# Turning gathered expert rows by DMA transposes of 16-bit halves in a four-layer attention and mixture-of-experts kernel

## The chip, the cores and the metric

The kernel runs on one core of one Trainium2 chip. The metric is the device time of one execution in microseconds (us), taken as the median of three runs. The profile is one further execution, recorded by the hardware profiler.

## The reference

Four layers act on x (8 batches of 256 tokens of width 256), each as x = x + layer(layernorm(x)). The first two are a correlation attention and a feed-forward layer with assigned experts, the third is a cross attention. The change lies wholly in the fourth, a mixture of 8 experts of inner width 1024 with the two best experts per token and a shared expert beside them:

```python
probs = jax.nn.softmax(logits, axis=-1)
top_v, top_i = jax.lax.top_k(probs, K)          # K = 2 of 8 experts
gates = jnp.zeros((T, e)).at[jnp.arange(T)[:, None], top_i].set(top_v)
g = jax.nn.silu(jnp.einsum('td,edf->etf', flat, w1_e))
u = jnp.einsum('td,edf->etf', flat, w3_e)
out_e = jnp.einsum('etf,efd->etd', g * u, w2_e)
routed = jnp.einsum('te,etd->td', gates, out_e).reshape(b, s, d)
return 0.5 * shared + 0.5 * routed
```

Everything is 32-bit float.

## The kernel before

**The mixture's stages.** While the third layer runs, each token's normalised row, its 8 gates and its own number (a row of `ROW` = 265 words) are sent by indirect DMA into the table `Td` in DRAM, sorted by expert. The mixture then works through `NBLK` = 11 blocks in one loop (L3796). Blocks 0 and 1 are the shared expert on two groups of 512 tokens, blocks 2 to 9 are the experts 0 to 7 with up to 512 rows each, and block 10 is the shared expert on the last group. Rows of an expert beyond 512 are worked on by the generator `slots` (L3598), one step of which is put between two units, from (2,1) on until it is done.

**Units.** A block is four up units, called (b,0) to (b,3) below, and one down unit. The order is (b,0), the down unit of block b-1, (b,1), (b,2), (b,3), then (b+1,0). Each unit is a product of 2 by 2 blocks in seven multiplications instead of eight, in three accumulators in PSUM: `a`, `e` (two buffers each) and `B` (two). `run_unit` (L3407) writes out the order by hand. TensorE's seven steps are A11 into a, S1 into e, then the *last* step of the unit before it (A22 into that unit's a, in `end_open`, L3399), S2 into a, A12 into B, S4 into e, S3 into a. Between them stand the reads: ScalarE's copies `seed` (L3221), `read_p5` and `read_u2`; VectorE's sums `read_c12` and `read_c22` (L3255) into the tile `cc`; and, after the A22 step, VectorE's `mult_2` (L3271), `read_last` (L3276) and `act_sums` (L3173) on the unit before. The lists `early`, `amid`, `late` and `after` are further steps that `run_unit` places after the A22 step, after A12, after S4 and after S3.

**Order of the engines.** The whole part stands under a manual schedule (L1256): every engine, SP's DMA queue included, runs its instructions in the order of the program. Waits are put in by the framework: an instruction that rewrites a buffer waits for all that still read it, and a DMA counts as reading until it has completed.

**Rows of an expert.** `load_rows` (L3489) loads the 512 rows of an expert into `R` (one buffer, 128 partitions by 4 rows by 265 words) through SP. `Turned` (L3497) turns them round, so that the width lies on the partitions: `half(kc)` does four TensorE transposes of 128x128 into PSUM (L3509) and one ScalarE copy to the tile `RT` (L3512). After the first half VectorE copies the token numbers into `ids` (L3514) and the gates into `gts` (L3515), both with three buffers. `Rows.steps` (L3146) then makes four sums of blocks of `RT` on VectorE. All of this lies in the down unit of block b-1, for the block n = b+1, and for expert 0 in unit (1,3).

**Result of an expert.** The down unit of an expert, `RoutedDown` (L3347), scales its four groups of 128 rows by the gates into `Y` and adds each to the output in DRAM, `Od`, by an accumulating indirect DMA that GpSimd issues (`add_rows`, L3517), with a column of `ids` as row numbers. The adds of groups 0 and 1 are issued in `read_c12` of the down unit, those of groups 2 and 3 in `read_last`, which comes in unit (b,1). As all write `Od`, each waits for the one before it to complete.

**Weights.** `load_up` (L2903) and `load_down` (L2921) load an expert's weights through SP, into tiles with two buffers each; `load_slots` (L3582) loads quarters of the weights for `slots`. The sums of the weights lie in parts of two older tiles: `SW` in the front of `HP` (L3758) and `TW` in the first six rows of `X` (L3761). The rows `lrows` of `X` (the last group of tokens) have been stored to `Od` before the loop (L3711) and are read back in block 10 (L3847).

Of the kernel before, what the change touches and what calls it, by code (L numbers as in the profile page):

```python
# [9 lines left out]
F32 = mybir.dt.float32  # L10
BF16 = mybir.dt.bfloat16
U32 = mybir.dt.uint32
I32 = mybir.dt.int32
AF = mybir.ActivationFunctionType
ALU = mybir.AluOpType
# [4 lines left out]
P = 128  # L20
LN_EPS = 1e-5
CAP1 = 576
FIRST = 512
# [1063 lines left out]
def fast_path(  # L1087
# [33 lines left out]
    nc = tc.nc  # L1121
    B, S, D = x.shape
    T = B * S
    NT = T // P
    KC = D // P
    TPB = S // P
    E = L0_ffn_w1.shape[0]
# [22 lines left out]
    X = res.tile([P, NT, D], F32, name="X")  # L1150
# [3 lines left out]
    ROW = D + E + 1  # L1154
# [13 lines left out]
    ident = const.tile([P, P], F32, name="ident")  # L1168
# [93 lines left out]
    pm = l0.enter_context(tc.tile_pool(name="pm", bufs=2))  # L1262
# [34 lines left out]
    for dst, src, i in (  # L1297
# [12 lines left out]
        out=bqd.rearrange("o (b c) -> (o b) c", b=B),  # L1310
        in_=L0_xattn_bq.partition_broadcast(B),
    )
    nc.scalar.dma_start(
        out=WZ[:, :, DH : 2 * DH],
        in_=L0_xattn_Wq.rearrange("(kc p) c -> p kc c", p=P),
# [267 lines left out]
    for h in range(TPB):  # L1583
# [36 lines left out]
        out=tri,  # L1620
        in_=tri,
# [26 lines left out]
    for sign, base in ((1, 1), (-1, 16)):  # L1648
        nc.gpsimd.affine_select(
            out=rows_f,  # L1650
            in_=rows_f,
# [33 lines left out]
    for r in range(2):  # L1685
        (nc.sync if r == 0 else nc.scalar).dma_start(
            out=Gd[0, 0 : S * W2].rearrange(
                "(tt p r w) -> p tt r w", p=P, r=2, w=S
            )[:, :, r, :],
            in_=G,  # L1690
# [4 lines left out]
        out=DG,  # L1695
        in_=Gd[0, :].rearrange("(tt p w) -> p tt w", p=P, w=W2 + 1)[:, :, 1 : S + 1],
# [53 lines left out]
    for tt in range(2):  # L1750
# [3 lines left out]
    rest = pa.tile([P, S], F32, name="rest")  # L1754
# [4 lines left out]
        out=rest, in_to_replace=top[:, 0, :], in_values=pcorr, imm_value=-3.0e38  # L1759
# [16 lines left out]
        out=Wd[:, 0:W2].rearrange("o (r s) -> o r s", r=2),  # L1776
        in_=wrow.unsqueeze(1).to_broadcast([P, 2, S]),
# [4 lines left out]
        out=CW,  # L1782
        in_=bass.AP(wd.tensor, wd.offset + P - 1, [[WD - 1, P], [P, 2], [1, S]]),
# [186 lines left out]
    sums = pa.tile([P, NT, 2], F32, name="sums")  # L1970
# [50 lines left out]
    halves = [slice(m * S, (m + 1) * S) for m in range(2)]  # L2021
# [7 lines left out]
    b = order_b  # L2029
# [101 lines left out]
    def load_row(e):  # L2131
# [14 lines left out]
        out=Yd.rearrange("(c p) d -> p c d", p=P),  # L2146
        in_=blank[:, 0:D].unsqueeze(1).to_broadcast([P, NT, D]),
# [300 lines left out]
    for e in range(E - 1):  # L2448
        if e == 5:

            wpv = L1_xattn_Wp.rearrange("(c g m d) n -> m g d c n", c=NB, g=4, m=2)
            for m in range(2):
                for g in range(4):
# [3 lines left out]
                        out=bvc[r0 : r0 + DH, :],  # L2457
                        in_=bkv[:, 1, :].rearrange("(c g m) d -> m g d c", c=NB, g=4)[m, g],
# [70 lines left out]
    ps_m = banks.enter_context(tc.tile_pool(name="ps_m", bufs=3, space=PSUM))  # L2529
# [436 lines left out]
    for b in range(B):  # L2966
        for c in range(NB):
# [55 lines left out]
            if prev is None:  # L3023
# [12 lines left out]
                HP = pg1.tile([P, NT, ROW], F32, name="HP")  # L3036
# [20 lines left out]
    FULL = FIRST // P  # L3057
# [7 lines left out]
    lrows = slice(LAST * (TB // P), NT)  # L3065
    HT2 = TB // 2
    HF = F // 2
# [17 lines left out]
    class UpWeights:  # L3085


        def __init__(self, wab, sums, s1=None):
            self.sums = sums
            self.raw = {  # L3090
                (h, kc): wab[:, :, kc, h * HF : (h + 1) * HF]
                for h in range(2)
                for kc in range(KC)
            }
            self.part = {
                A11: self.raw[0, 0],
                A12: self.raw[0, 1],
                A22: self.raw[1, 1],
                S1: self.raw[1, 0] if s1 is None else s1,
                S3: sums[:, :, 0],  # L3100
                S2: sums[:, :, 1],
                S4: sums[:, :, 2],
            }
# [120 lines left out]
    class Up(Unit):  # L3224
        n = TB
# [56 lines left out]
    class Down(Unit):  # L3282
        n = HT2
# [123 lines left out]
    def run_unit(u, early=(), amid=(), late=(), after=()):  # L3407

        before = open_unit[0]
        u.mm(u.a, A11, "b11", True)  # L3410
        u.seed()
        if before is not None:
            before.silu_2()
        u.mm(u.e, S1, "t1", True)
        u.read_p5()
        end_open()
        for do in early:
            do()
        u.mm(u.a, S2, "t2")
        u.read_u2()  # L3420
        u.mm(u.b, A12, "b21")
        for do in amid:
            do()
        u.mm(u.e, S4, "b22")
        u.read_c12()
        for do in late:
            do()
        u.mm(u.a, S3, "t3")
        u.read_c22()
        for do in after:  # L3430
            do()
        open_unit[0] = u
# [56 lines left out]
    def load_rows(e):  # L3489
        R = pe2.tile([P, FULL, ROW], F32, tag="R", name="R", bufs=1)  # L3490
        nc.sync.dma_start(
            out=R,
            in_=Td[e * CAP1 : e * CAP1 + FIRST, :].rearrange("(r p) w -> p r w", p=P),
        )
        return R

    class Turned:  # L3497


        def __init__(self, e, R):  # L3500
            self.e, self.R = e, R
            self.RT = pe2.tile([P, KC, FIRST], F32, tag="RT", name="RT")
            self.ids = pe2.tile([P, FULL], U32, tag="ids", name="ids", bufs=3)
            self.gates = pe2.tile([P, FULL], F32, tag="gts", name="gts", bufs=3)

        def half(self, kc):
            pt = ps_m.tile([P, FULL, P], F32, tag="pm", name="pt")
            for r in range(FULL):
                nc.tensor.transpose(  # L3509
                    pt[:, r, :], self.R[:, r, kc * P : (kc + 1) * P], ident  # L3510
                )
            nc.scalar.copy(self.RT[:, kc, :], pt.rearrange("p r q -> p (r q)"))  # L3512
            if kc == 0:
                nc.vector.tensor_copy(self.ids, self.R[:, :, ROW - 1])  # L3514
                nc.vector.tensor_copy(self.gates, self.R[:, :, D + self.e])  # L3515

    def add_rows(Y, ids):  # L3517
        nc.gpsimd.indirect_dma_start(  # L3518
# [164 lines left out]
    pe2 = ctx.enter_context(tc.tile_pool(name="pe2", bufs=2))  # L3683
# [83 lines left out]
    NBLK = 2 + E + 1  # L3767
# [3 lines left out]
    turned = {}  # L3771

    def up_unit(b, k):
        u = Up(ups[b], xs_[b], k, acts.setdefault(b, []))
        u.with_sums = b < NBLK - 1
        return u

    def down_unit(b):
        if b < 2:
            return SharedDown(downs[b], acts.pop(b), b + 1)  # L3780
        t = turned.pop(b)
        return RoutedDown(downs[b], acts.pop(b), t.gates, t.ids)
# [13 lines left out]
    for b in range(NBLK):  # L3796


        n = b + 1
        rest = ups[b].steps(P, HF) if b >= 2 else []  # L3800
        run_unit(up_unit(b, 0), after=rest[:2])
        if b == 0:
            Rs[2] = load_rows(0)
        if b >= 2 and b - 1 < E:
            W_up[b - 1] = load_up(w1p, b - 1)
        halves = []
        if 2 <= n < NBLK - 1:
            t = turned[n] = Turned(n - 2, Rs.pop(n))
            xs_[n] = Rows(t.RT)
            halves = [lambda: t.half(0), lambda: t.half(1)]  # L3810
        sums = xs_[n].steps() if n < NBLK else []
        if b > 0:
            late = b == 1
            run_unit(
                down_unit(b - 1),
                early=([] if late else halves[:1]) + rest[2:],
                amid=[] if late else halves[1:],
                late=[] if late else sums,
            )
        if 2 <= b < E:  # L3820
            Rs[b + 2] = load_rows(b)
        for k in range(1, NK):
            early, amid, after = [], [], []
            if k == 1 and 2 <= n < NBLK:
                ups[n] = UpWeights(WS[0] if n == NBLK - 1 else W_up.pop(n - 2), SW)
                after = ups[n].steps(0, P)
            if 2 <= b < NBLK - 1:
                if k == 2:
                    downs[b] = DownWeights(W_down.pop(b - 2), TW)
                    after = downs[b].steps()[:2]  # L3830
                if k == 3:
                    after = downs[b].steps()[2:]
            if b == 0:
                after = ([assign_slots], sums, shared_down.steps())[k - 1]
            if b == 1 and k == 3:
                early, amid, after = halves[:1], halves[1:], sums
            run_unit(up_unit(b, k), early, amid, after=after)
            if k == 1:
                if b >= 2 and b - 1 < E:
                    W_down[b - 1] = load_down(w1p, b - 1)  # L3840
                if b == 1:
                    flags()
                    experts = slot_experts()
                if b == 2:
                    beside = slots()
                if b == NBLK - 1:
                    nc.sync.dma_start(out=X[:, lrows, :], in_=odv[:, lrows, :])  # L3847
                    nc.sync.dma_start(
                        out=out.rearrange("b s d -> (b s) d")[0 : LAST * TB, :],
                        in_=Od[0 : LAST * TB, :],  # L3850
                    )
            if beside is not None and (b, k) != (2, 2):
                next(beside, None)
        if b == 1:
            Rs[3] = load_rows(1)
    last_down(WS[1], acts.pop(NBLK - 1))
    order.close()

# [51 lines left out]
```

## Time and profile before

| | before |
|---|---|
| median of 3 runs | 831.47 us (831.3 to 833.34) |
| the profiled execution | 830.43 us, span 828.7 us |
| TensorE busy | 806.3 us, 97% of the span |
| VectorE busy | 522.3 us, 63% |
| ScalarE busy | 348.7 us, 42% |
| GpSimd busy | 216.8 us, 26% |
| mean granted TensorE clock | 0.998 |
| all blocks with experts | about 430 to 800 us of the span |

The span is the time from the first to the last instruction. A busy share is a mean over stages with different limits, so a stage is read from the order of its instructions in time and from the chain of work that ended last. In lines of instructions, `out<-in` names the tiles written and read, `xN` counts instructions, and a bracket gives the idle time before and what seems to have ended it. PE is TensorE, PEld its weight loads, DVE VectorE, ACT ScalarE, POOL GpSimd, SPq the queue of DMAs that SP issues.

### The profile page before, as it was taken

The numbers are of one execution on the slowest core, as the hardware profiler recorded it, in microseconds if no ns is written. First come the engines' busy times: TensorE is split into PE (matmuls) and PEld (weight loads), VectorE is DVE, ScalarE is ACT, GpSimd is POOL, SyncE is SP. The second block draws the span as 40 slices with busy tenths as digits, with TensorE's granted clock in tenths as the row PEclk, the third lists the DMA queues.
The fourth block names the chain that finished last, engine by engine and source line by source line (L and its number), as shares of the span: only waits on it lengthen the run. The fifth ranks groups of instructions, "written<-read, shape, count | busy, mean of one in ns | idle before, by whom it ended". The sixth has DMA issues, their size and how long they took to land.

```text
span 828.7 us, 13872 instructions
## 1 busy us (share of the span) xinstructions
PE 806.3 (97%) x5188; PEld 636.2 (77%) x5188; DVE 522.3 (63%) x1470; ACT 348.7 (42%) x720; POOL 216.8 (26%) x293
## 2 busy tenths in 40 slices
PE   7999999999999999999999999999999999999997
PEld 6546787778745555557898989797979798999996
DVE  6377877440456586555775866767676758586731
ACT  4344454324377777431333233333333433443430
POOL 6251131230125455452330000202111232112020
PEclk9999999999999999999999999999999999999999
DMA  8395567942160000042120474656575754311023
GB/s 261 97 277 177 178 207 224 297 158 84 51 178 15 14 1 28 34 168 89 67 67 26 142 242 135 190 168 187 172 199 161 201 167 122 105 13 20 8 35 124
DMA packets 87316, 105.40 MB, mean 127 GB/s; under 512 B 9000, under 2 KB 77832, under 8 KB 87208
## 3 DMA queue, kind: packets, MB, share of 16 engines
q1 hardware_dynamic: 78568, 91.10, 35.0%
q0 software_dynamic: 7920, 13.02, 7.2%
q8 instruction: 43, 0.70, 0.4%
q10 hardware_dynamic: 752, 0.30, 0.1%
q14 instruction: 33, 0.27, 0.1%
HBM read 80.61 MB, written 25.37 MB: 128 GB/s over the span
## 4 chain that ended last, share of the span: by engine, by line
PE 88%; DMA 5%; DVE 3%; POOL 2%; ACT 1%; issue 1%; ACTq 0%; SPq 0%; DVEq 0%; POOLq 0%
PE a L3234 18%; PE e L3234 9%; PE a L3293 9%; PE py L2389 6%; PE ph L2372 5%; PE B L3234 5%; PE e L3293 4%; PE p L2652 4%; PE py L3439 3%; PE pv L2667 3%; PE B L3293 2%; PE pp L2718 2%; DMA R<-NMd,ids 2%; PE pgt L3196 2%; PE pp L2619 2%; PE pu L3196 2%
## 5 line engine op out<-in xcount | busy, mean ns | idle before, releaser
L3518 POOL DMA_INDIRECT Od<-Y,ids x32 | 51.6, 1612 | 300.5 <-DVE T L3083 184.0
L3222 ACT COPY B<-a 128x512 f32<-128x512 f32 (+1 forms) x54 | 28.6, 531 | 180.5 <-PE a L3234 142.6
L2660 ACT ACTIVATE ex<-p,scale 128x512 f32<-128x512 f32 x128 | 77.2, 689 | 27.5 <-PE p L2652 26.3
L3234 PE MATMUL a<-T,HP 128*128 128x256 f32 x288 | 73.9, 379 | 0.0
L3083 DVE TENSOR_TENSOR cc<-e,s 128x512 f32<-128x512 f32 x44 | 30.4, 691 | 58.0 <-PE e L3234 58.0
L3234 PE MATMUL a<-RT,wab 128*128 128x256 f32 x256 | 66.6, 383 | 0.0
L3083 DVE TENSOR_TENSOR act<-act 128x256 f32<-128x256 f32 (+1 forms) x120 | 61.4, 512 | 2.7
L2372 PE MATMUL ph<-RT,w 128*128 128x256 f32 x256 | 61.7, 389 | 0.8 <-ACT RT L2359 0.7
L2389 PE MATMUL py<-w,A 128*128 128x256 f32 x256 | 61.6, 388 | 0.0
L3234 PEld LDWEIGHTS a<-T,HP 128*128 128x128 f32 x288 | 54.0, 190 | 7.0
L3234 PEld LDWEIGHTS a<-RT,wab 128*128 128x128 f32 x256 | 46.4, 190 | 8.4 <-issue 1.6
L2381 ACT ACTIVATE A<-ph,b1c 128x256 f32<-128x256 f32 x64 | 30.0, 472 | 53.9 <-PE ph L2372 50.6
L2372 PEld LDWEIGHTS ph<-RT,w 128*128 128x128 f32 x256 | 45.3, 190 | 8.9 <-ACT A L2381 1.1
L2389 PEld LDWEIGHTS py<-w,A 128*128 128x128 f32 x256 | 46.6, 190 | 6.4
L2892 POOL DMA_INDIRECT Td<-HP,to x32 | 32.9, 1030 | 56.9 <-DMA Td<-HP,to 51.6
L2652 PE MATMUL p<-QM,KT 32*128 32x512 f32 x256 | 43.4, 640 | 0.4 <-DVE QM L2633 0.4
L3083 DVE TENSOR_TENSOR act<-act,cc 128x512 f32<-128x512 f32 x44 | 30.4, 691 | 17.6 <-ACT act L3268 17.1
L2399 POOL DMA_INDIRECT Yd<-Y,ids x16 | 15.7, 984 | 81.9 <-DVE Y L2398 49.0
L2667 PE MATMUL pv<-ex,VA 128*32 128x256 f32 x512 | 34.5, 385 | 0.2 <-DVE ov L2677 0.2
L3249 ACT COPY s<-a 128x512 f32<-128x512 f32 x44 | 25.7, 585 | 20.4 <-PE a L3234 20.4
L2667 PEld LDWEIGHTS pv<-ex,VA 128*32 128x32 f32 x512 | 13.5, 109 | 27.0 <-issue 11.7
L3234 PE MATMUL e<-T,wab 128*128 128x256 f32 x128 | 33.0, 380 | 0.3 <-DVE T L3083 0.3
(525 smaller groups left out, 1745.0 us busy)
## 6 DMA issues: line engine op xcount, KB each, us to landing
w<-in_L_ffn_w_dram SPq DMA_DIRECT2D x16, 1024.0 KB, 6.0
wab<-in_L_ffn_w_e_dram SPq DMA_DIRECT2D x16, 1024.0 KB, 4.9
wc<-in_L_ffn_w_e_dram SPq DMA_DIRECT2D x8, 1024.0 KB, 5.4
sab<-in_L_ffn_w_e_dram SPq DMA_DIRECT2D x32, 256.0 KB, 2.9
R<-Td SPq DMA_DIRECT2D x8, 530.0 KB, 3.7
sc<-in_L_ffn_w_e_dram SPq DMA_DIRECT2D x16, 256.0 KB, 2.8
Td<-blank SPq DMA_DIRECT2D x2, 1590.0 KB, 10.2
X<-in_x_dram SPq DMA_DIRECT2D x4, 512.0 KB, 5.3
```

What stands on the lines that cost most here:

```text
L2372: nc.tensor.matmul(ph, w1[:, kc, f * P : (f + 1) * P], RT[:, kc, :], start=(kc == 0), stop=(kc == KC - 1),)
L2381: nc.scalar.activation(A[:, f, :], ph, AF.Gelu_apprx_tanh, bias=b1c[:, e, f : f + 1])
L2389: nc.tensor.matmul(py, A[:, f, r * P : (r + 1) * P], w2[:, f, :], start=(f == 0), stop=(f == NF - 1),)
L2652: nc.tensor.matmul(ps[g].rearrange("p m q -> p (m q)"), KT[rows, c, k0 : k0 + P], QM[b][rows, c].rearrange("p m q -> p (m q)"), start=True ...
L2660: nc.scalar.activation(e4[:, g], ps[g], AF.Exp, scale=scale)
L2667: nc.tensor.matmul(pvs[b, c][32 * g : 32 * g + 32, m, :], VA[:, b * TPB + kt, 8 * c + 2 * g + m, :], ex[b, c, kt][:, g, m, :], start=(kt = ...
L2892: nc.gpsimd.indirect_dma_start(out=Td, out_offset=bass.IndirectOffsetOnAxis(ap=to[g][:, k, j : j + 1], axis=0), in_=HP[:, GT * g + j, :], ...
L3083: eng.tensor_tensor(out, a, b, op)
L3196: nc.tensor.matmul(ps, wab[:, m, kc, fs], xs[kc], start=(kc == 0), stop=(kc == KC - 1),)
L3234: nc.tensor.matmul(ps[:, m * HT2 : (m + 1) * HT2], self.w.get(m, left, self.k), self.x.part[right], start=start and m == 0, stop=True, ski ...
L3293: nc.tensor.matmul(ps[:, qs], self.acts[k][:, left, qs], self.w.get(right, k), start=start and i == 0 and k == 0, stop=(k == NK - 1), skip ...
L3518: nc.gpsimd.indirect_dma_start(out=Od, out_offset=bass.IndirectOffsetOnAxis(ap=ids, axis=0), in_=Y, in_offset=None, compute_op=ALU.add,)
```

## The change

The TensorE transposes of the gathered rows, their PSUM tiles and the two copies out of PSUM are gone. In their place each expert gets: two ScalarE copies (`take_apart`) that split two rows each into their lower and upper 16-bit halves, written into the unused rows `lrows` of `X`; four DMA transposes of 16-bit elements that SP issues, each 128 partitions by 512 elements, into a part of `HP` behind `SW`; and two ScalarE copies (`join`) that interleave the halves again into `RT`.

The places move too. `Turned` is now made at the start of unit (b,3) for block b+2, that is one block earlier than before (for expert 0 in unit (1,1), for expert 1 in unit (1,3)). Its constructor copies `ids` and `gts` on VectorE at once, ahead of the unit. `take_apart` and the DMA transposes stand in `amid` of that unit; `join` stands in `early` of the down unit in the next block (for expert 0 in `early` of unit (1,3)). The load of the rows for block 3 moves from the end of block 1 to just after unit (1,1). The tags `ids` and `gts` keep three buffers, `RT` two, `R` one.

```diff
     class Turned:
         def __init__(self, e, R):
-            self.e, self.R = e, R
-            self.RT = pe2.tile([P, KC, FIRST], F32, tag="RT", name="RT")
             self.ids = pe2.tile([P, FULL], U32, tag="ids", name="ids", bufs=3)
             self.gates = pe2.tile([P, FULL], F32, tag="gts", name="gts", bufs=3)
-
-        def half(self, kc):
-            pt = ps_m.tile([P, FULL, P], F32, tag="pm", name="pt")
-            for r in range(FULL):
-                nc.tensor.transpose(
-                    pt[:, r, :], self.R[:, r, kc * P : (kc + 1) * P], ident
-                )
-            nc.scalar.copy(self.RT[:, kc, :], pt.rearrange("p r q -> p (r q)"))
-            if kc == 0:
-                nc.vector.tensor_copy(self.ids, self.R[:, :, ROW - 1])
-                nc.vector.tensor_copy(self.gates, self.R[:, :, D + self.e])
+            nc.vector.tensor_copy(self.ids, R[:, :, ROW - 1])
+            nc.vector.tensor_copy(self.gates, R[:, :, D + e])
+            self.R = R
+            self.RT = pe2.tile([P, KC, FIRST], F32, tag="RT", name="RT")
+            self.parts = X[:, lrows, :].bitcast(U16)
+            self.turned = (
+                HP.rearrange("p n r -> p (n r)")[:, 2 * 3 * HF : 2 * 3 * HF + KC * FIRST]
+                .bitcast(U16)
+                .rearrange("p (c q) -> p c q", q=FIRST)
+            )
+
+        def take_apart(self, i):
+            two = slice(2 * i, 2 * i + 2)
+            nc.scalar.copy(
+                self.parts[:, two].rearrange("p r (t d) -> p r t d", t=2),
+                self.R[:, two, 0:D].bitcast(U16).rearrange("p r (d t) -> p r t d", t=2),
+            )
+            for r in (2 * i, 2 * i + 1):
+                nc.sync.dma_start_transpose(
+                    out=self.turned[:, :, r * P : (r + 1) * P],
+                    in_=self.parts[:, r],
+                )
+
+        def join(self, kc):
+            nc.scalar.copy(
+                self.RT[:, kc, :].bitcast(U16).rearrange("p (q t) -> p q t", t=2),
+                self.turned[:, kc : kc + 3 : 2, :].rearrange("p t q -> p q t"),
+            )
...
-        halves = []
-        if 2 <= n < NBLK - 1:
-            t = turned[n] = Turned(n - 2, Rs.pop(n))
+        joins = []
+        if 3 <= n < NBLK - 1:
+            t = turned[n]
+            joins = [lambda: t.join(0), lambda: t.join(1)]
             xs_[n] = Rows(t.RT)
-            halves = [lambda: t.half(0), lambda: t.half(1)]
-        sums = xs_[n].steps() if n < NBLK else []
+        sums = xs_[n].steps() if n < NBLK and b != 1 else []
         if b > 0:
-            late = b == 1
-            run_unit(
-                down_unit(b - 1),
-                early=([] if late else halves[:1]) + rest[2:],
-                amid=[] if late else halves[1:],
-                late=[] if late else sums,
-            )
+            run_unit(down_unit(b - 1), early=rest[2:] + joins, late=sums)
...
+            if b == 1 and k == 1 or 1 <= b < E and k == 3:
+                m = n if k == 1 else n + 1
+                t = turned[m] = Turned(m - 2, Rs.pop(m))
+                amid = [lambda: t.take_apart(0), lambda: t.take_apart(1)]
+            early = []
             if b == 1 and k == 3:
-                early, amid, after = halves[:1], halves[1:], sums
+                early = [lambda: turned[n].join(0), lambda: turned[n].join(1)]
             run_unit(up_unit(b, k), early, amid, after=after)
+            if b == 1 and k == 1:
+                Rs[3] = load_rows(1)
+            if b == 1 and k == 3:
+                xs_[n] = Rows(turned[n].RT)
+                for do in xs_[n].steps():
+                    do()
...
-        if b == 1:
-            Rs[3] = load_rows(1)
```

More of the change, by code (lines that the diff above doesn't have):

```diff
@@ L12 @@
 U32 = mybir.dt.uint32
+U16 = mybir.dt.uint16
 I32 = mybir.dt.int32
@@ L3822, in fast_path @@
         for k in range(1, NK):
-            early, amid, after = [], [], []
+            amid, after = [], []
             if k == 1 and 2 <= n < NBLK:
```

## The prediction

> **What bounds the kernel now.** I read the page's engine line first, then the chain that ended last for the stage of the mixture (440 to 830 us), then the order in time of one block.
>
> ```profile
> PE 806.3 (97%) x5188; PEld 636.2 (77%) x5188; DVE 522.3 (63%) x1470; ACT 348.7 (42%) x720; POOL 216.8 (26%) x293
> ```
>
> ```profile
> by line: PE a L3234 34.5%; PE e L3234 17.1%; PE a L3293 16.7%; PE B L3234 8.6%; PE e L3293 8.2%; PE B L3293 4.1%; PE py L3439 3.5%; PE pgu L3634 1.9%; PE pt L3509 1.8%; PE pys L3654 1.0%; PE pt L3648 0.2%; DVE cc L3083 0.2%; DVE X L3448 0.1
> ...
> 703.07 1.78 PE a L3293 x16
> ...
> 717.25 1.78 PE a L3293 x16
> ...
> 740.62 1.78 PE a L3293 x16
> ...
> 753.93 1.78 PE a L3293 x16
> ```
>
> TensorE is the chain almost without a gap, so whatever leaves it is gained. The last four lines are the first and last steps of two down units. The first holds two groups of transposes (L3509) and takes 717.25 - 703.07 = 14.18 us, the second holds none and takes 13.31. So a group of four costs 0.435 us, not 4 x 273 ns: matmuls overlap. It agrees with the chain's 1.8% of 390 us = 7.0.
>
> Now unit (4,3), where the change puts its new work, in order of time (start, us, engine):
>
> ```profile
> 569.99 1.03 PE L3234 MATMUL a<-RT,wab 128*128 128x256 f32 x4
> 570.58 1.28 DVE L3083 TENSOR_TENSOR X<-wc 128x512 f32<-128x512 f32 x2
> 571.78 0.41 DVE L3650 COPY aT<-pt 128x256 f32<-128x256 f32 x1
> 572.20 0.69 DVE L3083 TENSOR_TENSOR act<-act,cc 128x512 f32<-128x512 f32 x1
> 572.83 1.55 POOL L3518 DMA_INDIRECT Od<-Y,ids  x1 [6.26 <-ACT act L3259]
> 573.64 0.58 ACT L3249 COPY s<-a 128x512 f32<-128x512 f32 x1 [0.44 <-PE a L3234]
> 576.23 0.69 DVE L3083 TENSOR_TENSOR cc<-a,s 128x512 f32<-128x512 f32 x1
> 577.12 1.13 PE L3234 MATMUL a<-RT,wab 128*128 128x256 f32 x4
> 578.96 1.03 PE L3234 MATMUL a<-RT,wab 128*128 128x256 f32 x4
> ```
>
> 572.20 is `mult_2`, the first thing VectorE does for this unit. The POOL line is the *last of the four adds* of the expert of block 3, and it starts after that. It completes, and VectorE's load in this stretch is:
>
> ```profile
> L3518 POOL DMA_INDIRECT Od<-Y,ids x1: 1549/1549/1549, 572.8 to 572.8; - x1
> DMA to landing us min/median/max: 3.8/3.8/3.8
> ```
>
> ```profile
> 571.00:578.00 7.00, 7.00 (x45) 5.44 (x44) 6.51 (x13) 2.73 (x6) 1.55 (x1) 1.00 0.50 129
> ```
>
> The third busy figure is VectorE: 6.51 of 7.00 us, 93%, though it has 63% in the whole span. ScalarE, the fourth, has 2.73.
>
> **What the Trainium skill says.** "VectorE: DVE Perf Modes", The three transpose paths, gives 390 ns for a 128x128 transpose on TensorE and 1309 ns by DMA (both 16-bit). The trace shows 273 ns for one on TensorE and 109 ns each in a group, so the first figure is no price here. "Advanced Engine Details and Errata", X-Bar Transpose (TRN2), says transposing DMAs are as fast as regular ones; no run shows one yet. "ScalarE: Activation LUTs", What ACT_TABLE_LOAD costs, prices a ScalarE instruction at 186 ns + 0.833 ns an element: 0.61 us for 512, and the trace has 0.585 (L3512), 5% less. "DMA: Bandwidth & Descriptors", Rules for kernel authors, asks that an accumulating DMA wait for the one before it: the four adds do go one after another, 554.26, 559.06, 565.02, 572.83.
>
> **Removed: TensorE's transposes.** 16 groups (8 experts, two each) x 0.435 = **-6.96 us**, all on the chain. The 16 copies out of PSUM (0.585) leave ScalarE, where they cost nothing.
>
> **Added on ScalarE.** Four copies of 1024 elements per expert. From the row of 512, 0.585 + 512 x 0.833 ns = 1.01 us each; the other end, if 2-byte strides halve the rate, 2.0. `take_apart`: `read_u2` ends at 574.22 and the next ScalarE work is the seed at 578.29 (3.1 us between them in units without a step of `slots`): 2.0 us fit, cost 0. If 4.0, the seed is up to 0.9 late; S2, which rewrites what the seed reads, starts 1.7 us after A11 ends and the seed takes 0.57, so 1.1 can be spared: still 0. `join` in the down unit: ScalarE is free at 588.3, so the joins end at 590.4, and `read_u2`, otherwise at 590.1 (589.7 without the transposes), ends near 591.0. TensorE needs it for S3, two steps of 1.79 us later, near 593.1: cost 0 (at 2.0 us each, 593.0: just 0). For expert 0 both meet in (1,3): ScalarE is free at 453.2, the joins push `read_u2` to 455.8, S3 would start at 456.0 - 0.87 = 455.1: **+0.7 us**, once.
>
> **Added on SP.** 32 transposing DMAs of 128 KB, four per expert, behind `take_apart`. Nearest rows: 256 KB store Od<-X 2.1 us, 256 KB weights 2.8 us to landing. As regular DMAs four of them end 4 to 6 us after their start near 575.3; the join comes at 588.3, so cost 0. The dear end: 16 tiles of 1309 ns one after another (an estimate from the VectorE page) is 20.9 us. What they are moved past on SP: `sc` weights (577.26) and `wab` (580.01), which is first read at 602 to 604; 4 us of delay cost nothing. Below zero: no, SP is on no chain here. R's load leaves its place after the transposes and finds `R` free, no gain since TensorE did not wait for it.
>
> **Moved: the copy into `ids`.** This is the step that I hold to decide. With three buffers, block m takes the buffer of block m-3. Before, the copy stood in the down unit, one block after the last add of m-3. Now it stands at the start of (b,3) for m = b+2, and the adds of block m-3 = b-1 belong to this same block b. The copy must wait for the completion of all four adds, the last of which has just been issued. It is first in VectorE's queue: `mult_2`, `read_last`, `act_sums`, `read_c12`, `read_c22` all stand behind it.
>
> Who waits for those: TensorE's A22 step for this unit, the third of the next (578.96 above), rewrites the accumulator that `read_c22` reads. From 572.20 the queue to the end of `read_c22` takes 4.35 us without its idle gap (2.97 to the end of `act_sums`, two `cc` sums), and `ids` and `gts` 0.25. So TensorE resumes at landing + 0.3 (semaphore to engine; bounds 0 and 0.75, as the next add starts 0.75 after a landing) + 4.6. Per block, add's start + landing + 4.9 against the A22 step's time now (each read from the same two rows as above, or two steps after the next unit's A11):
>
> - block 3: 532.95 + 3.7 + 4.9 = 541.55; 537.8: 3.7
> - block 4: 572.83 + 3.8 + 4.9 = 581.53; 578.9: 2.7
> - block 5: 613.61 + 4.0 + 4.9 = 622.51; 619.9: 2.6
> - block 6: 654.16 + 3.8 + 4.9 = 662.86; 660.9: 1.9
> - block 7: 692.57 + 4.0 + 4.9 = 701.47; 698.6: 2.9
>
> Sum **+13.8 us** (bounds 12.3 and 16.0). Blocks 1 and 2 take fresh buffers. After this step VectorE is still late by some us, but the following down unit gives it room (9.50 busy of 14.00 us in 584 to 598), so it is not paid twice. The chain of adds starts in the down unit and is paced by its own landings, so it does not run ahead when TensorE is held.
>
> **Moved: the load for block 3.** It goes out behind four transposes at about 447 and lands near 451 (R<-Td, 3.7 us); VectorE reaches the copy at 451.5, and has 1.2 us to spare against TensorE: 0, up to 3 if the transposes hold SP.
>
> **Sum.** 830.43 - 6.96 + 13.8 + 0.7 = 838.0 for the profiled execution, which lies 1.04 below the median: **839.0 us**, 0.9% slower. About 0.3% (2.5 us) is what a measurement of this kernel can tell from no change.
>
> **Rivals.**
> *The copy is released early* (faster). If the wait ends when POOL has taken the indices, 1.55 us after the add starts, VectorE resumes 2.5 us sooner: the five costs become 1.3, 0.1, 0.1, 0 and 0.3, together 1.8, and the time is 831.5 - 7.0 + 0.7 + 1.8 = 827.0. The point from which it decides: a release within 2.6 us of the add's start (then the five cost less than the 6.3 gained). For it: little of the copy's work needs the finished sum. Against: the index tile is an operand of the DMA.
> *Half of that* (no change): adds that land sooner, since `R`'s load no longer falls among them, or VectorE's slack larger than I read: a loss of 4 to 9 us, 829 to 834.
> *Late transposes* (slower still). At 20.9 us the four end at 596.2, the joins at 598.2, `read_u2` at 598.9, against S3 at 593.1 + 2.7: 3.1 us for each of seven experts and 11 for expert 0, 33 in all: 872. It decides above some 15 us for four. For it: the page's 1309 ns; against: the other page. Shorter delays give 845 to 872.
>
> **Chances.** Forecast (834 to 845) 0.53; early release (below 829) 0.18; half 0.13; late transposes 0.16. So faster 0.18, same 0.13, slower 0.69. The range runs from 827 (half of the early-release case lies below) to 852 (half of the late case above), which leaves out 0.17. The slower cases alone run from 834.
>
> **What would show it.** Right: no L3509 rows; VectorE idle 4 to 6 us ahead of the `ids` copy in (3,3) to (7,3), ended by a DMA Od<-Y,ids; TensorE idle 2 to 4 us before the A22 step in the unit after, ended by `cc`; down units of 13.3 us. Wrong: no such idle time, then the early release; ScalarE idle ahead of the joins on a DMA, then the late transposes; seeds late by more than 1 us, then the copies were dearer than 2 us.

## The result, and the profile after

| | before | after |
|---|---|---|
| median of 7 runs each, us | 833.34 (831.3 to 834.85) | 838.07 (837.56 to 840.82) |
| profiled execution: time, span, us | 830.43, 828.7 | 838.07, 836.4 |
| mean granted TensorE clock of that execution | 0.998 | 0.992 |

The changed kernel takes 1.0065 times as long (95% interval 1.0047 to 1.0084): 5.4 us more, between 3.9 and 7.0. The lines below answer to those of the prediction, in its order; line numbers have moved by 1 in the units, by more below them. First the page's engine line.

```profile
PE 803.6 (96%) x5124; PEld 631.5 (76%) x5124; DVE 520.2 (62%) x1470; ACT 371.7 (44%) x736; POOL 216.4 (26%) x293
```

TensorE has 64 instructions fewer, the transposes, and its busy share fell from 97 to 96% all the same: idle time has come in. Next the chain that ended last, 440 to 830 us: its shares by line, and the first and last step of one down unit.

```profile
by line: PE a L3235 33.1%; PE a L3294 17.1%; PE e L3235 15.7%; PE e L3294 8.2%; PE B L3235 8.0%; PE B L3294 4.1%; PE py L3440 3.4%; DMA Od<-Y,ids 3.1%; PE pgu L3652 1.9%; DVE act L3084 0.9%; DVE cc L3084 0.8%; PE pys L3672 0.8%; issue 0.7%;
...
584.80 1.78 PE a L3294 x16
...
598.11 1.78 PE a L3294 x16
```

The transposes' 1.8% are gone, and this down unit takes 598.11 - 584.80 = 13.31 us. In their place stands what is not among the shares of before: `DMA Od<-Y,ids` with 3.1% of 390 us. Unit (4,3) in order of time shows how an accumulating DMA gets onto TensorE's path (start, us, engine; in brackets the idle time before it and what ended it):

```profile
572.15 1.55 POOL L3536 DMA_INDIRECT Od<-Y,ids  x1 [2.94 <-DVE cc L3084]
...
574.64 0.58 ACT L3250 COPY s<-a 128x512 f32<-128x512 f32 x1 [0.44 <-PE a L3235]
575.12 2.00 ACT L3519 COPY X<-R 128x1024 uint16<-128x1024 uint16 x2
...
575.95 0.17 DVE L3506 CAST ids<-R 128x4 uint32<-128x4 f32 x1 [2.73 <-DMA Od<-Y,ids]
576.02 0.17 DVE L3507 COPY gts<-R 128x4 f32<-128x4 f32 x1
576.10 0.69 DVE L3084 TENSOR_TENSOR act<-act,cc 128x512 f32<-128x512 f32 x1
...
576.19 5.12 SPq L3524 DMA_TRANSPOSE HP<-X  x4
...
578.12 1.13 PE L3235 MATMUL a<-RT,wab 128*128 128x256 f32 x4
...
580.22 1.13 PE L3235 MATMUL a<-RT,wab 128*128 128x256 f32 x4
```

The add starts at 572.15 and lands 3.8 us later, at 575.95; at 575.95 VectorE starts the copy into `ids`, after 2.73 us with nothing to do, and `mult_2` (576.10) comes behind it. SP then gives 5.12 us to the four transposes. From 571 to 578 VectorE is busy for 4.23 us, where it had 6.51:

```profile
571.00:578.00 7.00, 7.00 (x46) 5.53 (x44) 4.23 (x11) 4.63 (x8) 1.55 (x1) 1.00 0.26 36
```

All such waits of 440 to 800 us (total, times, longest):

```profile
DVE ids L3506 <- DMA Od<-Y,ids: 19.7, 5, 9.5
...
PEld a L3235 <- DVE act L3084: 9.2, 5, 7.3
PE a L3235 <- DVE act L3084: 7.1, 2, 6.9
...
DVE ids L3506 <- DMA R<-Td: 1.2, 1, 1.2
```

Five waits, as there are blocks 3 to 7, but not five alike: they are 1.71, 2.73, 3.63, 2.15 and 9.49 us. TensorE feels the second and the third a little (the table below) and the last one fully:

```profile
698.02 1.55 POOL L3536 DMA_INDIRECT Od<-Y,ids  x1 [3.03 <-DMA Od<-Y,ids]
702.39 0.17 DVE L3506 CAST ids<-R 128x4 uint32<-128x4 f32 x1 [9.49 <-DMA Od<-Y,ids]
...
703.94 2.08 PE L3235 MATMUL a<-RT,wab 128*128 128x256 f32 x4 [6.93 <-DVE act L3084]
...
705.81 1.65 PE L3235 MATMUL e<-T,wab 128*128 128x256 f32 x4
...
707.29 1.03 PE L3235 MATMUL a<-RT,wab 128*128 128x256 f32 x4
```

**Where the time went.** The start of each down unit on TensorE says it best. The table has the time from one down unit's first step to the next one's, so each row holds one (b,3) with its wait; the loss is what exceeds the before's interval less the 0.87 us that two groups of transposes took.

| (b,3) between | before | after | loss |
|---|---|---|---|
| (3,3) | 41.04 | 40.16 | 0 |
| (4,3) | 41.04 | 40.53 | 0.36 |
| (5,3) | 41.03 | 41.42 | 1.26 |
| (6,3) | 41.04 | 40.16 | 0 |
| (7,3) | 37.56 | 45.39 | 8.7 |

From the down unit at 463.59 us (before) to the end of the mixture this makes 7 x -0.87 + 10.3 = +4.2 us. Block 1 before it came out even: 0.87 less and 0.9 more in (1,3). Another 3.6 us of the profiled pair lie ahead of the change: unit (1,1) begins its A11 at 440.49 in place of 436.90, after code that is the same in both. Of these, 1.6 come at one place: from 103 to 106 us the granted clock of the changed kernel's profile was 0.50, and that of the kernel before was not. The change's own cost in the pair is thus 4.2 us, close to the 4.7 between the medians.

### The profile page after: what moved, and what is told of

Read it like the earlier page. It is cut to its first block, busy times and chain, and to the rows that moved or that the text cites. A ratio compares the mean times of both kernels' runs of the same rounds, so it can differ in the third digit from the quotient of the medians.

```text
span 836.4 us, 13830 instructions
## 1 busy us (share of the span) xinstructions
PE 803.6 (96%) x5124; PEld 631.5 (76%) x5124; DVE 520.2 (62%) x1470; ACT 371.7 (44%) x736; POOL 216.4 (26%) x293
## 4 chain that ended last, share of the span: by engine, by line
PE 84%; DMA 6%; DVE 4%; ACT 2%; POOL 2%; issue 1%; ACTq 0%; SPq 0%; DVEq 0%; POOLq 0%
PE a L3235 18%; PE a L3294 9%; PE e L3235 8%; PE py L2390 6%; PE ph L2373 6%; PE e L3294 4%; PE B L3235 4%; PE p L2653 4%; PE py L3440 3%; PE pv L2668 3%; PE B L3294 2%; PE pp L2719 2%; DMA R<-NMd,ids 2%; PE pgt L3197 2%; PE pp L2620 2%; PE pu L3197 2%
## 5 line engine op out<-in xcount | busy, mean ns | idle before, releaser
L3250 ACT COPY s<-a 128x512 f32<-128x512 f32 x44 | 25.8, 586 | 20.1 <-PE a L3235 20.1
```

## Experiments

The runs are called by their numbers here. Each kernel's ratio is against the kernel before, run beside it on the same chip: 830.47 us for runs 1, 3, 4 and 5, 829.43 for runs 2, 6, 7 and 8. A down unit's interval is read as in the table above; undisturbed it is 40.16 us, and 36.68 around (7,3).

**1. A fourth buffer.**

```
-            self.ids = pe2.tile([P, FULL], U32, tag="ids", name="ids", bufs=3)
-            self.gates = pe2.tile([P, FULL], F32, tag="gts", name="gts", bufs=3)
+            self.ids = pe2.tile([P, FULL], U32, tag="ids", name="ids", bufs=4)
+            self.gates = pe2.tile([P, FULL], F32, tag="gts", name="gts", bufs=4)
```

> The changed kernel with four buffers for ids and gts in place of three; nothing else differs. Theory A (the moved copy into ids waits for the last adds of the same block, and TensorE behind it): the idle time of VectorE ahead of that copy (19.7 us in five waits) and the 10.3 us that TensorE lost in blocks 4, 5 and 7 go; about 838.1 - 10.3 = 828 us, some 5 us faster than the kernel before, and the granted clock stays at full speed near block 7. Theory B (the transposing DMAs on SP, or ScalarE's copies, cost the time): no change, 838 us, and TensorE still waits in those blocks.

824.0 us (823.36 to 825.46), ratio 0.9927 (0.9912 to 0.9941). Of the waits of 440 to 800 us these are left for the copy and for TensorE's first tile:

```profile
PEld a L3235 <- DVE cc L3084: 1.8, 5, 0.4
...
PEld a L3235 <- ACT s L3250: 1.0, 1, 1.0
DVE ids L3506 <- DMA R<-Td: 0.9, 1, 0.9
...
PE a L3235 <- ACT s L3250: 0.6, 1, 0.6
```

No copy waits for an add and no `mult_2` holds TensorE. The intervals are 40.16, 40.17, 40.15, 40.17 and 36.68 us: each the before's less 0.87. The buffer that the copy waits for is the whole of the loss; without that wait the change is a gain of 6 us.

**2. Which of the two buffers.** Only `ids` gets four; `gates` keeps three.

> The changed kernel with four buffers for ids alone; gates keep three. Only ids is read by the accumulating DMAs, gates by ScalarE when Y is drained, long before. Theory A (the index tile is the one that is held until the add has landed): all of the gain of four buffers for both, so 824 us and no wait of the copy of ids or of gates. Rival (gates are held as well, by the units that drain Y late): a wait of gates appears in its place and the time lies between 826 and 838.

824.71 us (823.39 to 825.55), ratio 0.9938 (0.9921 to 0.9954), with no wait of either copy for anything but `R`. It is the index tile that is held until the add has landed; the gates tile, read by ScalarE and VectorE when `Y` is made (L3354, L3363), was free in time.

**3. The copies alone.** The kernel before, with TensorE's transposes where they were, and only the two copies moved, from block 4 on to the start of (b,3):

```
+            nc.vector.tensor_copy(self.ids, R[:, :, ROW - 1])
+            nc.vector.tensor_copy(self.gates, R[:, :, D + e])
...
-            if kc == 0:
-                nc.vector.tensor_copy(self.ids, self.R[:, :, ROW - 1])
-                nc.vector.tensor_copy(self.gates, self.R[:, :, D + self.e])
...
+            if n not in turned:
+                turned[n] = Turned(n - 2, Rs.pop(n))
+            t = turned[n]
...
+            if 2 <= b < E and k == 3:
+                turned[b + 2] = Turned(b, Rs.pop(b + 2))
```

> The kernel before with only the copies into ids and gts moved: for blocks 4 to 9 they stand at the start of unit (b,3) for block b+2, as in the changed kernel, with three buffers; the transposes stay on TensorE. Theory A with the prediction's own sizes: five waits of 4 to 6 us ahead of the copy in blocks 3 to 7, TensorE loses 3.7, 2.7, 2.6, 1.9 and 2.9 us, 13.8 in all: about 847 us against 833. Theory B: no change.

845.23 us (843.86 to 851.0), ratio 1.019 (1.0164 to 1.0216). Its waits:

```profile
DVE ids L3505 <- DMA Od<-Y,ids: 22.6, 5, 5.0
...
PEld a L3234 <- DVE act L3083: 8.6, 5, 2.0
PE a L3234 <- DVE act L3083: 6.3, 5, 1.6
PEld a L3234 <- DVE cc L3083: 5.8, 6, 1.1
PE a L3234 <- DVE cc L3083: 3.6, 5, 0.7
```

Five waits, none over 5.0 us, and all five reach TensorE: its intervals lose 2.6, 1.8, 2.6, 2.3 and 2.6 us, 11.8 in all. The prediction had 3.7, 2.7, 2.6, 1.9 and 2.9 for them: right in kind and within 1.1 us each. So alone the copy costs what was forecast, less 2.0; inside the change it costs 10.3 and lies elsewhere. Something else in the change moves the adds.

The edit does one thing more, which the expectation leaves out: the copies for experts 0 and 1 now stand ahead of a down unit, and that of expert 0 waits 6.5 us for `R` there. TensorE loses 2.1 us in that unit, the one ahead of (1,1). So the 845.23 us, near the 847 expected, hold 2.1 us of another origin.

**4. The transposes behind the loads.** The changed kernel with three buffers, but from block 2 on SP issues the transposes after the step of loads that follows (b,3), so that the slots' and shared expert's loads keep the place that they had. (In block 1 they go out right behind their units.)

```
-            for r in (2 * i, 2 * i + 1):
+
+        def turn(self):
+            for r in range(FULL):
...
+            if 2 <= b < E and k == 3:
+                t.turn()
```

> The changed kernel, three buffers, but from block 2 on the four transposing DMAs are issued after the step of slots that follows unit (b,3), so that SP issues the quarter's weights (sab) as early as in the kernel before. Theory C (SP, held by the transposes, sends these weights out 18 us later, away from the adds, which is why the last add of blocks 3 to 6 lands earlier than before): with the loads back, the second and third add of a block take 6 to 7 us again, the waits ahead of the ids copy in blocks 3 to 6 return to 4 to 6 us, TensorE loses 2 to 4 us in each; in block 7 the late loads no longer delay the adds of slots and the wait falls from 9.5 to about 4 us. Sum of TensorE's losses about 13.8 in place of 10.3: some 841 us. Rival: the later loads cost time themselves, then below 838.

841.27 us (835.83 to 843.23), ratio 1.0114 (1.0087 to 1.0142).

```profile
DVE ids L3506 <- DMA Od<-Y,ids: 26.1, 5, 9.4
```

In (3,3) to (6,3) TensorE now loses 1.9, 3.7, 1.3 and 0.9 us, 7.8 in place of the change's 1.6 (1.8 of the 7.8 is a slow clock after the wait in (4,3), see the end), and block 4's adds are back at 553.72, 558.41, 565.41 and 573.21, as before the change. That part came as expected: it is SP's order that made the last adds of these blocks land earlier. The part on block 7 failed. Its wait was to fall to about 4 us and stayed at 9.4, and TensorE lost 10.0 us there. That the time is the 841 expected is therefore chance.

**5. Both.** Four buffers, and the transposes behind the loads.

> Four buffers and the transposing DMAs behind the loads of slots. Theory A: no wait ahead of the ids copy, 828 us as with four buffers alone, since the place of the loads mattered only through the adds. If the displaced loads cost something by themselves, this one is faster than four buffers alone.

825.77 us (824.47 to 827.39), ratio 0.9941 (0.9927 to 0.9954), its intervals 40.17, 40.16, 40.16, 40.16 and 36.68. With the wait gone, SP's order is worth nothing in these intervals. The median is 1.8 us above that of run 1; between the two profiles 3.5 us of difference lie ahead of unit (1,1), where the kernels are the same. In block 2 the transposes now go out so late that a join waits for them, which dates their landing (a line from SP, one from ScalarE):

```profile
502.20 5.70 SPq L3526 DMA_TRANSPOSE HP<-X  x4
```

```profile
509.40 2.23 ACT L3532 COPY RT<-HP 128x1024 uint16<-128x1024 uint16 x2 [0.94 <-DMA HP<-X]
```

The four have landed 7.2 us after the first was issued, 1.5 us after SP is through with the last. TensorE loses nothing by it. (Run 4 has the same wait, as long.)

**6. Why block 7.** What is special there is that the slots' four small adds stand ahead of block 7's own on GpSimd. SP's queue of the kernel before, then of the changed one, in that stretch:

```profile
645.82 4.44 SPq L2911 DMA_DIRECT2D wab_-1_6540<-in_L_ffn_w_s_dram  x4
659.33 0.37 SPq L2924 DMA_DIRECT2D wc_-1_6545<-in_L_ffn_w_s_dram  x1
662.09 0.88 SPq L2916 DMA_DIRECT2D wab<-in_L_ffn_w_e_dram  x2
674.42 0.37 SPq L3491 DMA_DIRECT2D R<-Td  x1
```

```profile
658.14 5.65 SPq L3524 DMA_TRANSPOSE HP<-X  x4
663.88 4.51 SPq L2912 DMA_DIRECT2D wab_-1_6527<-in_L_ffn_w_s_dram  x4
668.49 1.67 SPq L2925 DMA_DIRECT2D wc_-1_6532<-in_L_ffn_w_s_dram  x1
670.27 2.21 SPq L2917 DMA_DIRECT2D wab<-in_L_ffn_w_e_dram  x2
672.57 0.42 SPq L3492 DMA_DIRECT2D R<-Td  x1
```

The slots' adds went out at 660.08, 665.52, 670.68 and 673.69 before, and at 660.95, 665.07, 671.24 and 677.70 after, where loads that had been spread over 29 us are issued in 9. The run leaves the slots' four adds out:

```
-                for g in range(SLOTS):
-                    add_rows(Y[g * SR : (g + 1) * SR, :], ids[:, g : g + 1])
```

> The changed kernel with three buffers as it is, but the four small accumulating DMAs that add the slots' 32-row results to the output are left out (part of the result is missing). Question: is block 7's wait of 9.5 us, three times that of the other blocks, made by the four small adds that stand ahead of block 7's own on GpSimd's queue, each taking its place behind the one before? Theory A (the queue of adds): the first of block 7's adds then goes out when its Y is ready, about 11 us after its down unit begins as in block 6 (677 in place of 684 us), the last lands about 7 us earlier, and the wait ahead of block 7's copy of the ids falls from 9.5 to between 2 and 5 us; with the slow clock after the long idle gone too, about 838 - 7 = 831 us. Rival (the shared expert's displaced weight loads slow all adds there, whoever they belong to): block 7's adds still take 7 us each, the wait stays above 7 us, and the time stays at 836 or more.

831.31 us (828.67 to 833.96), ratio 1.0014 (1.0 to 1.0028).

```profile
DVE ids L3506 <- DMA Od<-Y,ids: 15.3, 5, 4.9
...
PE a L3235 <- DVE act L3084: 3.0, 2, 2.4
```

Block 7's first add goes out at 675.24 in place of 684.17, which is 11.2 us after its down unit begins in place of 18.0. The longest wait is 4.9 us, and the interval around (7,3) is 41.01 in place of 45.39. Half of block 7's excess is thus the queue of small adds ahead of its own. The gain is 4.2 us by the ratios (0.5%), not the 7 expected.

The traces also show what is left. In this run block 7's last add goes out 27.8 us after its down unit begins, as block 6's does (27.2), and in block 6 that costs TensorE nothing. But `slots` has no work left in block 7, and an undisturbed interval there is 36.68 us, where around (6,3) it is 40.16. So VectorE comes to the copy sooner after the same adds: it waits 4.93 us, where it waits 1.92 in (6,3). TensorE then waits 2.4 us, and a slow clock adds 1.8 (see the end). No run tests this by itself.

**7. More of the transposes.** Four buffers, and the first two of each expert's transposes issued twice.

```
-            for r in (2 * i, 2 * i + 1):
+            for r in (2 * i, 2 * i + 1) * (2 - i):
```

> Four buffers for ids and gates, and the first two of each expert's four DMA transposes are issued twice (same values written again), so that SyncE is held some 2.5 us longer per expert and the transfers move half as much again. Theory A (with nobody waiting for the adds, SyncE's hold and the transposes' transfers lie beside other work): 824 us, within 1 us of four buffers alone. Rival (the weight loads behind the transposes have no slack left, or the joins come to wait for the transposes' landing): a new wait of ScalarE at the joins or of VectorE for weights, 1 to 2.5 us in each of six blocks, so 830 to 838.

826.71 us (824.08 to 828.42), ratio 0.996 (0.9945 to 0.9976): 2.0 us above run 2, which ran beside it. Neither expectation holds. Four of the blocks keep their 40.16 us. The loss is in block 1 (1.4), where the rows for block 3 load later and VectorE waits 3.4 us for them in place of 0.9, and around (7,3), 38.49 for 36.68 (one line from SP, one from VectorE):

```profile
653.81 10.69 SPq L3524 DMA_TRANSPOSE HP<-X  x6
```

```profile
684.13 0.48 DVE L3084 TENSOR_TENSOR HP<-wab 128x256 f32<-128x256 f32 x1 [2.81 <-DMA wab<-in_L_ffn_w_e_dram]
```

Six transposes hold SP for 10.69 us where four of run 1 held it for 6.17, more than the 2.5 us that I had added, and VectorE then waits 2.81 us for weights that stand behind them. The transposes themselves are never waited for by the joins. SP's hold is free as the change has it, with less than the added 4.5 us to spare at (7,3). The run moves half as many bytes again as well, so it does not part SP's hold from the transfers' share of the DMA engines.

**8. More on ScalarE.** Four buffers, and each taking apart and each join done twice.

```
+            for _ in range(2):
                 nc.scalar.copy(
```

> Four buffers for ids and gates, and each of ScalarE's two taking-apart copies and two joins of an expert done twice, so 4.4 us more of ScalarE per expert. Theory A (ScalarE has slack of about 2 us behind the taking apart and behind the joins in the stages from block 2 on, so that its copies are hidden there, and the only place without slack is block 1's last unit, where all four copies of two experts meet): 826 to 828, the addition being 2 to 4 us in block 1 and nothing after. Rival (the copies are only just hidden, and a second set lies on TensorE's path at the down units' drains of Y or at the gate's products): 1 to 2 us per block and 832 to 840 us.

830.43 us (829.23 to 833.39), ratio 1.001 (0.9997 to 1.0022): 5.7 us above run 2, above the first theory and below the rival. Its waits on TensorE in 440 to 800 us, the two that grew:

```profile
PE a L3235 <- ACT s L3250: 2.9, 1, 2.9
...
PEld a L3294 <- ACT Y L3354: 2.0, 6, 0.3
```

From unit (1,1) to the down unit before (4,3) it loses 3.6 us against run 1, most of it the idle time of 2.9 at one step of (1,3), as the first theory had it; but each later interval is 0.4 us longer too (40.57 for 40.16), and 0.7 around (7,3) (37.40 for 36.68), where the joins delay the drain of Y (the second line: 6 waits of at most 0.3). So the change's copies fit, and twice as much no longer does.

## Why the prediction came out as it did

The time on record, 839.0, stands against 838.07, but much of the agreement is chance. I forecast +7.5 us of change; the medians differ by 4.7, the ratio says 5.4 (3.9 to 7.0). The rest is that the before took 833.34 in these runs and not 831.47. And the +4.7 is near because two errors in the largest term go against each other: 9.3 us too much for (3,3) to (6,3), 5.8 too little for (7,3). By its own steps:

**TensorE's transposes, -6.96: right.** Seven down units give 0.87 each, in the changed kernel where nothing waits and in runs 1, 2 and 5 everywhere: -6.1 from the first of them to the end in all three. The eighth pair of groups, in (1,3), is eaten by the term after next.

**ScalarE's copies, 0: right.** A taking apart takes 1.05 us and a join 1.165, where I had 1.01 from "ScalarE: Activation LUTs", What ACT_TABLE_LOAD costs; the joining copy is 15% dearer than that estimate. I had put the limit at 2.0 us each in the down unit, "just 0"; at 2.3 (run 8) it costs 0.4. **(1,3), +0.7:** measured 0.9, the amount by which block 1 fails to show its 0.87 (the wait for `s`, L3250, in run 1).

**SP's transposes, 0: right for the joins, wrong for what is behind them.** They hold SP 5.1 to 5.8 us per expert, and in the changed kernel no join waits for them. Run 5 has them landed 7.2 us after the first issue, a little over the 4 to 6 forecast; the dear end of 20.9, worked from the 1309 ns of "VectorE: DVE Perf Modes", The three transpose paths, as a serial price, is out. "Advanced Engine Details and Errata", X-Bar Transpose (TRN2), has transposing DMAs as fast as regular ones, and the traces do not speak against it: in run 1 one of 128 KB lands 2.5 us after its issue (median), a store Od<-X of 256 KB 2.2 us.

What stands behind them I read wrongly. I listed `sc` (577.26) and `wab` (580.01), the loads that start after the transposes would. But SP had run ahead: the eight loads of `sab`, issued at 563.75 before, stand behind the transposes in the program too. SP runs its queue in order, and the transposes wait for `take_apart` in (4,3), so `sab` goes out at 581.57, 18 us later. And I asked only whether the delayed loads come in time for their readers, and not what they had been colliding with.

**The copy into `ids`, +13.8: the mechanism right, the size and the place wrong.** It waits for the landing to a tenth of a us (572.15 + 3.8 = 575.95), so the rival of an early release is refuted for this program. "DMA: Bandwidth & Descriptors", Two DMAs through the same engine are not ordered, says that a DMA's completion semaphore is the ordering an author has; here the tile that is waited for is only the DMA's list of indices, and the wait is as long. Runs 1 and 2 show that this one buffer is all of the loss, 10.3 us; run 3 prices it alone at 11.8.

The step that failed is "add's start + landing + 4.9", with the adds' starts taken from the kernel before. They did not stay. In blocks 3 to 6 SP's order moved the slots' weights away from the later adds: block 4's last three stand 4.5 us apart, where they had 6.0 and 7.8 (the first gap grew, from 4.8 to 8.0), and the last lies 2.55 us earlier against TensorE (572.15 with TensorE 1.87 late, against 572.83). So 10.9 forecast for (3,3) to (6,3) became 1.6; run 4 puts the order back and gets 7.8. In block 7 it went the other way, 8.7 for 2.9. I never looked at the slots' adds, which are in the same queue. Run 6 gives them half of it.

The 4.9 itself was near: in run 3 the A22 step starts 4.27 us after the copy, where 4.6 stood. But TensorE does not wait where I said, ahead of A22 for `cc`, alone. It stops first ahead of A11, which rewrites the accumulator `a` that the delayed `read_last` still reads: in run 3, 6.3 us in five waits there and 3.6 us in five ahead of A22; in the changed kernel's (7,3), all 6.93 ahead of A11.

**The load for block 3, 0 (up to 3):** VectorE waits 1.17 us for it; no loss of TensorE's can be put down to it. With SP held longer (run 7) it does cost, 1.4 us.

**The rivals.** No change: the nearest miss, for adds that do land sooner, but block 7 took the gain back. Late transposes: no join of the changed kernel waits for one, and the only waits, one each in runs 4 and 5, are of 0.94 us.

**What stays open.** Why an add is slow. The traces show what goes with it: in the profiles of the kernel before, of the change and of runs 1, 2, 3, 4 and 6, 137 adds of 128 rows between 500 and 720 us have a landing time. The 74 beside which less than 70 GB/s moved in their first 4 us landed in 3.6 to 4.2 us, the 44 beside more than 200 GB/s in 3.9 to 8.0, half of them over 6. That fits block 7 of run 4, whose second own add follows the first by 7.5 us (683.74 to 691.25): a load of 1 MB is issued at 684.27, 0.5 us behind the first add. So the loads are the likely cause, but no run takes a single load away.

I also did not settle all of why unit (1,1) begins between 0.8 us earlier and 3.6 later than in the before's profile, with the same code ahead of it (run 3 without its own 2.1 us). The profiles of the change and of runs 3, 5, 6 and 8, which are 1.0 us or more late there, each have 3.4 us of half clock near 100 us, where TensorE falls 1.6 us back; those of runs 1, 2, 4 and 7, and of the kernel before, do not. Why one execution has it and another not is open.

## What to carry to other kernels

When a step that writes a small tile moves earlier, ask which transfers still read the buffer's last contents: in this program an accumulating DMA holds its index tile until it has landed (3.8 us for the one in (4,3)), and a wait at the head of VectorE's queue delays everything behind it. Whether the DMA itself needs the tile that long, or only the wait that the framework sets, no run shows. One more buffer for the 128x4 row numbers (run 2) turned this change from 0.65% slower into 0.6% faster (0.5 to 0.8%), and is the version to keep. Before a wait on a chain of transfers is priced, work out the chain's times in the *changed* kernel: a new DMA on a queue also moves every load behind it, towards or away from that chain. What is behind it is told by the order of the program, not by the times in the trace: a queue that runs ahead issues loads early that a new entry ahead of them will hold back (here `sab`, by 18 us).

## What the runs showed that was not expected

Some waits of TensorE cost more than their length. In the changed kernel's (7,3) it had no work from 697.0 to 703.94. From 700 to 705 us the granted clock was 0.52 on the mean, from 705 to 710 it was 0.79 (the column ahead of the last two):

```profile
700.00:705.00 5.00, 1.06 (x3) 0.89 (x4) 2.54 (x8) 0.00 (x0) 0.00 (x0) 0.52 0.47 73
705.00:710.00 5.00, 5.00 (x20) 4.23 (x19) 4.93 (x10) 3.02 (x6) 0.00 (x0) 0.79 0.13 15
```

The first two groups of four matmuls took 2.08 and 1.65 us for 1.03, 1.7 us on top of the wait, which with its 6.93 makes up the 8.7 of the table but for 0.1. "TensorE: Matmul & The Clock Gate", Part 1, has it so: half the clock after some 3.4 us of idle time. The half agrees with the traces; the idle time does not, and here the measurement counts. In (4,3) of run 4 a wait of 1.92 us was enough:

```profile
578.57 1.34 PE L3235 MATMUL a<-RT,wab 128*128 128x256 f32 x4 [1.92 <-DVE act L3084]
```

```profile
575.00:580.00 5.00, 3.08 (x25) 1.91 (x24) 2.91 (x9) 0.63 (x2) 0.00 (x0) 0.94 0.65 150
580.00:585.00 5.00, 5.00 (x18) 3.91 (x18) 4.84 (x10) 2.86 (x6) 0.00 (x0) 0.72 1.12 170
```

The clock was 0.50 from 579.4 to 582.7, and three groups took 1.34, 1.91 and 1.72 us: 1.8 us more than the 1.13, 1.03 and 1.03 of such groups at full clock. In (7,3) of run 6 a wait of 2.37 us had the same sequel and cost 1.8 us more. The waits of 0.70 to 1.56 us in run 3 did not set it off: a group of four took 1.13 us after each of them. But near 100 us two waits of under 0.9 us, in 3 us of which TensorE was busy for half, were followed by it in the change's profile and not in the before's. So no single length of wait decides it here; what does, the runs do not show.
